# Layer 0's masked row maxima: a fused add-and-minimum on the Vector engine in place of mask products on the Tensor engine

## The chip, the cores and the metric

The kernel runs on one NeuronCore of a Trainium2 chip. A core has a Tensor engine (TensorE, PE in the profile; PEld is its weight loads), a Vector engine (DVE), a Scalar engine (ACT), a GpSimd engine (POOL) and a Sync engine (SP) that issues transfers. Products land in PSUM, which has eight banks of 128 partitions x 512 fp32 columns; everything else lives in SBUF. Each engine works through its own instructions in order and waits on semaphores for the others. The metric is the device time of one execution in microseconds; the time shown is the median of three runs.

## The reference, cut to what matters

The program is four layers over `x`, 16 batches of 256 tokens with 256 features. Layer 0 is self-attention with rotated queries and keys and a mask, cross-attention to 77 context tokens with a mask, and an MLP; layer 1 is a cross-attention; layer 2 is self-attention, cross-attention and an MLP; layer 3 is rotated self-attention, cross-attention and an MLP. All attentions have 16 heads of 16 features. The part that the change touches is the softmax of layer 0's self-attention:

```python
s = jnp.einsum('bqhd,bkhd->bhqk', q, k) * scale
s = jnp.where(mask, s, jnp.finfo(s.dtype).min)
a = jax.nn.softmax(s, axis=-1)
```

The mask is one 256 x 256 array of booleans, the same for all batches and heads. A softmax needs, for each query and head, the maximum of its masked scores over the 256 keys.

## The kernel before

**Stages.** `pixart_kernel` walks through the layers: stage "a" (layer 0's self-attention) and "ac" (its cross-attention), the MLP "b", then "cx", "c" and "cc" (layers 1 and 2), the MLP "d", then "e" and "ec" (layer 3) and the MLP "f". Each stage works on 16 batches, and `x` stays in SBUF. The function `attention` makes the tasks of one batch. It is called for every stage and takes `masked=True` only for "a" and "ac"; the stages "a", "c" and "e" are self-attentions (`self_` is true), and "a" and "e" rotate queries and keys.

**One self-attention batch.** Normalised `x` is turned, projected to queries and keys, rotated on DVE and POOL (lines 588 to 608), turned back (line 628) and copied out as `qT` and `kz`. `kz` holds the keys twice, with one of the two heads of each 32-row strip zeroed, so that one product of a 32-row strip gives the scores of two heads. Heads come in two groups `g` of eight (four strips of two heads), queries in two tiles `t` of 128. The strips are taken in two row pairs `rp`.

*Maxima.* For each `g`, `t` and `rp` one PE task (`begin`, line 734) takes two PSUM banks, one for each strip of the pair. In stage a it first writes the mask into both banks: the bf16 identity times the bf16 mask `mb`, 512 columns (the mask twice), line 740. `mb` is 0 where the mask is true and -2^120 where it is false. Then it adds the scores by a 32-row product of 512 columns, line 749. For each bank one DVE task reduces 128 x 512 to two negated maxima a row (line 772) and writes them into `mxt`. So there are 2 x 2 x 4 = 16 reductions a batch. When a group's eight are done, `mxt` is turned on PE (line 787) and put into the extended queries `qx` on DVE (line 792), where the maximum becomes an extra feature of the query.

*Exponentials.* The scores are computed a second time, keys in rows now and the maximum subtracted by the product itself (`begin`, line 821; product at line 834). The turned mask `mbT` is written into the banks first (line 827). ACT takes the exponential (line 848). The values product (line 857) sums over keys. DVE transposes the result (line 866), takes reciprocals (line 873), POOL multiplies, DVE transposes back (line 883), and the output projection follows (line 904), with the gate (line 917) and the residual (line 920).

**What sets the order.** No loop order is issued as it stands. Every step is a task with an engine, an estimated duration, dependencies and buffers, added to an `Order`; `solve` (line 101) plays a list schedule over these estimates, and the kernel issues the tasks in the order that comes out. `CAPS` gives the buffers of each kind: 8 banks ("b"), 2 maxima tiles, 4 batches' queries and keys. PE takes the ready task with the lowest priority number; the other engines take tasks that hold a bank first, then by the time at which they became ready. Two PE tasks that use different row pairs are started together and their products alternate (`choose`), since they use different rows of the array; `begin` of `Order` (line 125) gives such a pair one common duration, the longer of the two. In stage a the mask products raise both kinds of task, maxima and exponentials, from 0.864 to 1.614 in these estimates. Batches are admitted to an attention stage in the order in which they became ready.

The mask tiles `mb`, `mbT` and `kbm` (for "ac") live in a buffer of the kind "ctx", made at line 988 and the lines after it.

Of the kernel before, what the change touches and what calls it, by code (L numbers as in the profile page):

```python
# [10 lines left out]
F32 = mybir.dt.float32  # L11
# [6 lines left out]
P = 128  # L18
# [41 lines left out]

class Task:
    __slots__ = ("eng", "dur", "run", "deps", "take", "prio", "rp", "left", "ready", "outs", "held", "start", "end", "no", "since", "kind", "joins",
                 "line", "last")


class Hold:
# [7 lines left out]
class Order:  # L74
# [8 lines left out]
        self.caps, self.tasks = caps, []  # L83

    def add(self, eng, dur, run, deps=(), take=(), use=(), prio=0, rp=None, kind=None, joins=(),
            line=None, last=True):

        t = Task()
        t.joins, t.line, t.last = joins, line, last
        t.eng, t.dur, t.run, t.prio, t.rp, t.kind = eng, dur, run, prio, rp, kind  # L90
        t.deps = [d for d in deps if d is not None]
        t.take, t.held = list(take), list(take) + list(use)
        for h in t.held:
            h.users += 1
        t.outs, t.left, t.ready, t.no, t.since = [], len(t.deps), 0.0, len(self.tasks), None
        for d in t.deps:
            d.outs.append(t)
        self.tasks.append(t)
        return t

    def solve(self):
# [22 lines left out]

        def begin(ts):
            nonlocal seq, mode
            dur = max(t.dur for t in ts)
            if ts[0].eng == "PE":
                kind = "row" if ts[0].rp is not None else ts[0].kind
                dur += self.TURN.get(kind, 0.2) if kind != mode else 0.0  # L130
                mode = kind
            for t in ts:
                for h in t.take:
                    h.no = loose[h.tag].pop(0) if h.tag in loose else taken[h.tag]
                    taken[h.tag] += 1
                for name, key in t.joins:
                    lines.setdefault(name, []).append(key)
                if t.line is not None and t.last:
                    lines[t.line[0]].pop(0)
                t.start, t.end = now, now + dur  # L140
                waiting[t.eng].remove(t)
                seq += 1
                heapq.heappush(events, (now + dur, seq, t))
            if ts[0].eng != "NO":
                free[ts[0].eng] = now + dur
            result.append((now, len(result), ts))
# [60 lines left out]
def pixart_kernel(ctx: ExitStack, tc: tile.TileContext, x, cond_t, ctx_in, mask_c, mask_s, tables, vecs, rows,  # L207
# [427 lines left out]
    def attention(b, name, n, wv, wkeys, h_w, w_t, eps, mod, half, biases, masked, pre_add, gate, prio, ctxs=None,  # L635
# [85 lines left out]
        for g in range(NC):  # L721
            h_mx, h_x = Hold("mx"), Hold("qx")

            def open_mx(g=g):
                s["mx", g] = mxs[state["mx"] % len(mxs)]
                state["mx"] += 1
            t_mx = add("NO", 0.0, open_mx, deps=[q_t, k_t], take=[h_mx], prio=prio, line=("mx", (nm, g)))
            red = []
            for t in tiles:
                for rp in range(2):  # L730
                    hs = [Hold("b"), Hold("b")]
                    u = {}

                    def begin(g=g, t=t, rp=rp, u=u, hs=hs):
                        lists = []
                        for i in range(2):
                            r = 2 * rp + i
                            ps = u[i] = psum(hs[i])
                            if self_ and masked:
                                nc.tensor.matmul(ps.rearrange("p (s k) -> p s k", k=N), lhsT=identb,  # L740
                                                 rhs=mb[:, t, :].unsqueeze(1).to_broadcast([P, 2, N]),
                                                 start=True, stop=False)
                        for i in range(2):
                            r = 2 * rp + i
                            R = slice(32 * r, 32 * r + 32)
                            ps, ls = u[i], []
                            keys = s["kz"][R, g].rearrange("p s k -> p (s k)")
                            if self_:
                                ls.append(lambda ps=ps, R=R, keys=keys: nc.tensor.matmul(  # L749
                                    ps, lhsT=s["qT"][R, g, t * P:(t + 1) * P], rhs=keys,  # L750
                                    start=not masked, stop=True))
                            else:
                                pv = ps[:, 0:4 * n].rearrange("p (u k) -> p u k", k=n)
                                if masked:
                                    ls.append(lambda pv=pv, r=r: nc.tensor.matmul(
                                        pv, lhsT=onesb[32 * r:32 * r + 1, :],
                                        rhs=kbm[32 * r:32 * r + 1, b, :].unsqueeze(1).to_broadcast([1, 4, LC]),
                                        start=True, stop=False))
                                for tt in range(NT):
                                    ls.append(lambda ps=ps, R=R, keys=keys, tt=tt: nc.tensor.matmul(  # L760
                                        ps[:, 2 * tt * n:2 * (tt + 1) * n], lhsT=s["qT"][R, g, tt * P:(tt + 1) * P],
                                        rhs=keys, start=not masked, stop=not masked or tt == NT - 1))
                            lists.append(ls)
                        return lists
                    dur = 2 * MM if self_ else 0.55
                    a = add("PE", dur + (0.75 if self_ and masked else 0.0), begin, deps=[t_mx], take=hs,
                            use=[h_q, h_k, h_mx, *h_masks], prio=prio, rp=rp, kind="m")
                    for i in range(2):
                        def reduce(g=g, t=t, r=2 * rp + i, i=i, u=u):
                            m = s["mx", g]  # L770
                            if self_:
                                nc.vector.tensor_reduce(m[:, t, 32 * r:32 * r + 17:16],  # L772
                                                        u[i].rearrange("p (s k) -> p s k", k=N), AX.X, ALU.max,
                                                        negate=True)
                            else:
                                nc.vector.tensor_reduce(m[:, :, 32 * r:32 * r + 17:16],  # L776
                                                        u[i][:, 0:4 * n].rearrange("p (t s k) -> p t s k", s=2, k=n),
                                                        AX.X, ALU.max, negate=True)
                        red.append(add("DVE", 0.69 if self_ else 0.46, reduce, deps=[a], use=[hs[i], h_mx],
                                       prio=prio))  # L780
            hm, u2 = Hold("b"), {}

            def turn(g=g, u2=u2, hm=hm):
                u2["p"] = psum(hm)
                s["qx", g] = work.tile([P, 2, N], F32, tag="qx", bufs=CAPS["qx"], name=f"qx_{nm}_{g}")
                for t in range(NT):
                    nc.tensor.transpose(u2["p"][:, t * P:(t + 1) * P], s["mx", g][:, t, :], ident)  # L787

            def plus(g=g, u2=u2):
                qx = s["qx", g]  # L790
                for i in range(2):
                    nc.vector.scalar_tensor_tensor(qx[:, i, :], u2["p"][:, 0:N], spot[:, i:i + 1], s["qT"][:, g, :],
                                                   ALU.mult, ALU.add)
            a = add("PE", 2 * TR, turn, deps=red, take=[hm, h_x], use=[h_mx], prio=prio, line=("qx", (nm, g)))
            qx_t.append(add("DVE", 0.85, plus, deps=[a], use=[hm, h_x, h_q], prio=prio))
            h_qx.append(h_x)
# [7 lines left out]
        for g in range(NC):  # L804
            u5, h_av, h_so = {}, Hold("b"), Hold("ts")
            for kc in range(nk):
# [10 lines left out]
                for rp in (1, 0):  # L817
# [3 lines left out]
                    def begin(g=g, kc=kc, rp=rp, u=u, hs=hs):  # L821
# [8 lines left out]
                        for i in range(2):  # L830
# [6 lines left out]
                                    start=not (self_ and masked), stop=not (self_ and masked) or q == 1))  # L837
                                for q in range(2)])
                        return lists
                    a = add("PE", 2 * MM + (0.75 if self_ and masked else 0.0), begin,  # L840
                            deps=[t_e, k_t], take=hs, use=[h_k, h_qx[g], *h_masks], prio=prio, rp=rp, kind="e")
                    for i in range(2):
                        def exp(g=g, kc=kc, r=2 * rp + i, i=i, u=u):
# [143 lines left out]

    mask_t = work.tile([P, NC, CT], F32, tag="ctxT", bufs=CAPS["ctx"], name="ctxT_masks")
    mask_b = mask_t.rearrange("p c n -> p (c n)")[:, 0:1152].bitcast(BF16)
    mb, mbT = (mask_b[:, i * 512:(i + 1) * 512].rearrange("p (t n) -> p t n", n=N) for i in range(2))  # L990
    kbm = mask_b[:, 1024:1024 + CT].rearrange("p (b n) -> p b n", n=LC)

# [240 lines left out]
```

## Time and profile before

| | |
|---|---|
| median of three runs | 2854.78 us (2854.26 to 2854.85) |
| profiled execution | 2851.73 us, its span 2849.3 us |
| mean granted TensorE clock in it | 0.993 |
| PE busy | 2782.7 us, 98% of the span |
| DVE busy | 1651.1 us, 58% |
| ACT busy | 1205.4 us, 42% |
| POOL busy | 1062.6 us, 37% |
| line 740, mask products of the maxima | 256, 380 ns each in their rows |
| line 827, mask products of the exponentials | 256, 382 ns each |
| line 772, reductions, all three self-attentions | 768, 684 ns each |

How to read it: the profile is one execution. A busy PE is not a PE at its peak, since products are pipelined and the ends of their rows are modelled: rows overlap, so that the distance from one start to the next is shorter than a row. The same holds on DVE, where the next instruction starts some 70 to 80 ns before the row ahead of it ends. The span is the time from the first to the last instruction; the execution's own time has 2.4 us around it. Idle time of an engine that is not the bound costs nothing.

### The profile page before, as it was taken

The numbers are of one execution on the slowest core, as the hardware profiler recorded it, in microseconds if no ns is written. First come the engines' busy times: TensorE is split into PE (matmuls) and PEld (weight loads), VectorE is DVE, ScalarE is ACT, GpSimd is POOL, SyncE is SP. The second block draws the span as 40 slices with busy tenths as digits, with TensorE's granted clock in tenths as the row PEclk, the third lists the DMA queues.
The fourth block names the chain that finished last, engine by engine and source line by source line (L and its number), as shares of the span: only waits on it lengthen the run. The fifth ranks groups of instructions, "written<-read, shape, count | busy, mean of one in ns | idle before, by whom it ended". The sixth has DMA issues, their size and how long they took to land.

```text
span 2849.3 us, 55972 instructions
## 1 busy us (share of the span) xinstructions
PE 2782.7 (98%) x22560; PEld 1954.0 (69%) x22560; DVE 1651.1 (58%) x4042; ACT 1205.4 (42%) x2496; POOL 1062.6 (37%) x1414
## 2 busy tenths in 40 slices
PE   7999999999999999999999998999999999999999
PEld 4555555667788766656666666888656666666888
DVE  4656666677322267787777677111678888786110
ACT  1333343455333245545555554222444454443222
POOL 2332322254544444323333544343333333354331
PEclk9999999999999999999999999999999999999999
DMA  4010000000111100010000000100000000000000
GB/s 169 23 31 5 5 7 5 9 11 17 60 34 42 56 19 2 5 28 12 15 14 13 5 2 1 63 19 15 31 1 1 1 2 1 1 2 1 23 19 19
DMA packets 32034, 56.24 MB, mean 20 GB/s; under 512 B 3456, under 2 KB 22128, under 8 KB 31008
## 3 DMA queue, kind: packets, MB, share of 16 engines
q1 hardware_dynamic: 31776, 52.68, 5.8%
q8 instruction: 177, 2.90, 0.4%
q14 instruction: 81, 0.66, 0.1%
HBM read 48.34 MB, written 4.33 MB: 18 GB/s over the span
## 4 chain that ended last, share of the span: by engine, by line
PE 90%; DVE 4%; POOL 3%; ACT 1%; issue 1%; DMA 1%; SPq 0%; DVEq 0%; ACTq 0%; POOLq 0%
PE bank L904 18%; PE bank L834 12%; PE bank L947 12%; PE bank L857 11%; PE bank L749 7%; PE bank L540 6%; PE bank L588 5%; PE bank L706 5%; PE bank L451 3%; PE bank L787 2%; PE bank L827 2%; PE bank L760 2%; PE bank L740 2%; PE bank L628 1%; DVE mxt L772 1%
## 5 line engine op out<-in xcount | busy, mean ns | idle before, releaser
L772 DVE TENSOR_REDUCE mxt<-bank 128x2 f32<-128x512 f32 x768 | 484.8, 684 | 149.5 <-PE bank L749 138.5
L776 DVE TENSOR_REDUCE mxt<-bank 128x4 f32<-128x308 f32 x512 | 211.8, 470 | 35.4 <-PE bank L834 18.6
L848 ACT ACTIVATE e_a<-bank 128x512 f32<-128x512 f32 x256 | 136.7, 598 | 209.8 <-PE bank L749 147.0
L848 ACT ACTIVATE e_e<-bank 128x512 f32<-128x512 f32 x256 | 136.3, 603 | 161.9 <-PE bank L749 80.7
L848 ACT ACTIVATE e_c<-bank 128x512 f32<-128x512 f32 x256 | 135.6, 600 | 119.9 <-PE bank L749 83.6
L910 DVE TENSOR_TENSOR x_sb<-x_sb,bank 128x512 f32<-128x512 f32 x80 | 54.8, 685 | 189.1 <-PE bank L904 187.1
L749 PE MATMUL bank<-kz_c,qT_c 32*128 32x512 f32 x512 | 142.0, 627 | 0.0
L749 PE MATMUL bank<-kz_e,qT_e 32*128 32x512 f32 x512 | 137.0, 632 | 1.5 <-DVE kz_e L563 0.8
L834 PE MATMUL bank<-qx_e,kz_e 32*128 32x256 f32 x1024 | 134.6, 402 | 0.0
L834 PE MATMUL bank<-qx_c,kz_c 32*128 32x256 f32 x1024 | 132.5, 397 | 0.0
L834 PE MATMUL bank<-qx_a,kz_a 32*128 32x256 f32 x1024 | 122.6, 400 | 0.0
L749 PE MATMUL bank<-kz_a,qT_a 32*128 32x512 f32 x512 | 120.9, 640 | 0.0
L952 ACT ACTIVATE h_f<-bank,vec 128x256 f32<-128x256 f32 x128 | 53.5, 470 | 153.5 <-PE bank L947 132.5
L952 ACT ACTIVATE h_d<-bank,vec 128x256 f32<-128x256 f32 x128 | 53.5, 470 | 153.6 <-PE bank L947 132.5
L947 PE MATMUL bank<-xT_b,w_b 128*128 128x256 f32 x512 | 114.6, 380 | 0.0
L904 PE MATMUL bank<-w_b,h_b 128*128 128x256 f32 x512 | 113.7, 379 | 0.0
L904 PE MATMUL bank<-w_d,h_d 128*128 128x256 f32 x512 | 113.4, 380 | 0.0
L947 PE MATMUL bank<-xT_d,w_d 128*128 128x256 f32 x512 | 113.4, 380 | 0.0
L947 PE MATMUL bank<-xT_f,w_f 128*128 128x256 f32 x512 | 113.4, 380 | 0.0
L904 PE MATMUL bank<-w_f,h_f 128*128 128x256 f32 x512 | 113.2, 379 | 0.0
L714 ACT COPY vt<-bank 128x256 f32<-128x256 f32 (+1 forms) x160 | 54.7, 374 | 129.2 <-PE bank L706 118.1
L952 ACT ACTIVATE h_b<-bank,vec 128x256 f32<-128x256 f32 x128 | 53.5, 470 | 125.7 <-PE bank L947 83.4
(386 smaller groups left out, 6788.3 us busy)
## 6 DMA issues: line engine op xcount, KB each, us to landing
cin<-in_ctx_in_dram SPq DMA_DIRECT2D x36, 128.0 KB, 2.1
x_sb<-in_x_dram SPq DMA_DIRECT2D x16, 256.0 KB, 6.3
gb_b<-gate_g0m SPq DMA_DIRECT2D x16, 256.0 KB, 3.3
gb_c<-gate_g2a SPq DMA_DIRECT2D x16, 256.0 KB, 3.2
gb_d<-gate_g2m SPq DMA_DIRECT2D x16, 256.0 KB, 3.1
out_dram<-x_sb SPq DMA_DIRECT2D x16, 256.0 KB, 2.1
w_c<-in_wc_dram SPq DMA_DIRECT2D x1, 3072.0 KB, 9.9
w_e<-in_we_dram SPq DMA_DIRECT2D x1, 3072.0 KB, 10.1
```

Source lines behind the costliest of these rows:

```text
L540: nc.tensor.matmul(dst[:, g, :], lhsT=w[:, k, g * P:(g + 1) * P], rhs=xT[:, k, :], start=(k == 0), stop=(k == NC - 1))
L588: nc.tensor.matmul(u["p"][0:r, at:at + D], lhsT=xT()[:, k, t * P:t * P + r], rhs=w()[:, k, :], start=(k == 0), stop=(k == NC - 1))
L706: nc.tensor.matmul(ps[0:rows_n, t * D:(t + 1) * D], lhsT=xT[:, k, t * P:t * P + rows_n], rhs=wv[kv][:, k, :], start=(k == 0), stop=(k == N ...
L749: ls.append(lambda ps=ps, R=R, keys=keys: nc.tensor.matmul(ps, lhsT=s["qT"][R, g, t * P:(t + 1) * P], rhs=keys, start=not masked, stop=True))
L772: nc.vector.tensor_reduce(m[:, t, 32 * r:32 * r + 17:16], u[i].rearrange("p (s k) -> p s k", k=N), AX.X, ALU.max, negate=True)
L776: nc.vector.tensor_reduce(m[:, :, 32 * r:32 * r + 17:16], u[i][:, 0:4 * n].rearrange("p (t s k) -> p t s k", s=2, k=n), AX.X, ALU.max, neg ...
L834: (lambda ps=u[i], R=R, q=q: nc.tensor.matmul(ps[0:rows_n, q * N:(q + 1) * N], lhsT=s["kz"][R, g, q, kc * P:kc * P + rows_n], rhs=s["qx", ...
L848: nc.scalar.activation(e, u[i][0:rows_n], AF.Exp)
L857: nc.tensor.matmul(u5["p"][32 * r:32 * r + 32, 1 - q, :], lhsT=s["v"][0:rows_n, kc, 8 * g + 2 * r + 1 - q, :], rhs=s["e", g, kc, r][0:rows ...
L904: nc.tensor.matmul(u["p"][:, t, :], lhsT=lhsT(k, t), rhs=w()[:, k, :], start=(k == 0), stop=(k == nk - 1))
L947: nc.tensor.matmul(u["p"][:, j, :], lhsT=wv["w1"][:, k, f * P:(f + 1) * P], rhs=s["xT"][:, k, :], start=(k == 0), stop=(k == NC - 1))
L952: nc.scalar.activation(s["h", i][:, j, :], u["p"][:, j, :], func, bias=vcol(b1, 2 * i + j))
```

## The change

In stage a's maxima the mask products (line 740) go, and the score product starts its bank itself. In place of one reduction over both heads' 512 columns, DVE runs, for each head, `tensor_tensor_reduce` over 256 columns: it adds the mask tile `mb` (bf16, SBUF) to the scores (fp32, PSUM), multiplies by -1, writes the result to a scratch tile `junk`, and writes the minimum of it, started at 3e38, into the head's place in `mxt`. That is the negated maximum of the masked scores, as before. The masks of the exponentials stay on PE. The planner's estimates follow: the maxima task loses its 0.75, a masked reduction is estimated at 0.95 in place of 0.69, and a masked exponentials task carries 0.62 in a new field `more`, which is added for each task of a pair where the old 0.75 stood inside the longer task's duration.

```diff
@@ class Task, Order.add @@
-                 "line", "last")
+                 "line", "last", "more")
...
-            line=None, last=True):
+            line=None, last=True, more=0.0):
...
-        t.joins, t.line, t.last = joins, line, last
+        t.joins, t.line, t.last, t.more = joins, line, last, more
@@ Order.solve, begin @@
-            dur = max(t.dur for t in ts)
+            dur = max(t.dur for t in ts) + sum(t.more for t in ts)
@@ attention, maxima @@
                             ps = u[i] = psum(hs[i])
-                            if self_ and masked:
-                                nc.tensor.matmul(ps.rearrange("p (s k) -> p s k", k=N), lhsT=identb,
-                                                 rhs=mb[:, t, :].unsqueeze(1).to_broadcast([P, 2, N]),
-                                                 start=True, stop=False)
...
                                 ls.append(lambda ps=ps, R=R, keys=keys: nc.tensor.matmul(
                                     ps, lhsT=s["qT"][R, g, t * P:(t + 1) * P], rhs=keys,
-                                    start=not masked, stop=True))
+                                    start=True, stop=True))
...
                     dur = 2 * MM if self_ else 0.55
-                    a = add("PE", dur + (0.75 if self_ and masked else 0.0), begin, deps=[t_mx], take=hs,
+                    a = add("PE", dur, begin, deps=[t_mx], take=hs,
                             use=[h_q, h_k, h_mx, *h_masks], prio=prio, rp=rp, kind="m")
...
                             m = s["mx", g]
-                            if self_:
+                            if self_ and masked:
+                                for i2 in range(2):
+                                    nc.vector.tensor_tensor_reduce(
+                                        junk, u[i][:, i2 * N:(i2 + 1) * N], mb[:, t, :], -1.0, 3.0e38, ALU.add, ALU.min,
+                                        m[:, t, 32 * r + 16 * i2:32 * r + 16 * i2 + 1])
+                            elif self_:
                                 nc.vector.tensor_reduce(m[:, t, 32 * r:32 * r + 17:16],
                                                         u[i].rearrange("p (s k) -> p s k", k=N), AX.X, ALU.max,
                                                         negate=True)
...
-                        red.append(add("DVE", 0.69 if self_ else 0.46, reduce, deps=[a], use=[hs[i], h_mx],
+                        red.append(add("DVE", 0.95 if self_ and masked else 0.69 if self_ else 0.46, reduce, deps=[a], use=[hs[i], h_mx],
                                        prio=prio))
@@ attention, exponentials @@
-                    a = add("PE", 2 * MM + (0.75 if self_ and masked else 0.0), begin,
+                    a = add("PE", 2 * MM, begin, more=0.62 if self_ and masked else 0.0,
                             deps=[t_e, k_t], take=hs, use=[h_k, h_qx[g], *h_masks], prio=prio, rp=rp, kind="e")
@@ set-up @@
+    junk = const.tile([P, N], F32, name="junk")
```

## The prediction

> **What bounds the kernel now.** I read the page's busy shares first, then the chain of waits over the layer-0 self-attention, then windows of steady work, then single groups. The page gives the engines over the whole span:
>
> ```profile
> PE 2782.7 (98%) x22560; PEld 1954.0 (69%) x22560; DVE 1651.1 (58%) x4042; ACT 1205.4 (42%) x2496; POOL 1062.6 (37%) x1414
> ```
>
> TensorE is the bound nearly everywhere, so the question is whether it stays so in the stage that changes. That is the self-attention "a" of layer 0. The first and last starts of its maxima products (line 749), beside those of layer 3's "e", which has the same rotated queries and keys but no mask, are:
>
> ```profile
> L749 PE MATMUL bank<-kz_a,qT_a x512: 587/640/692, 49.7 to 532.0; 32*128 32x512 f32 x171
> ...
> L749 PE MATMUL bank<-kz_e,qT_e x512: 587/588/692, 2017.8 to 2382.6; 32*128 32x512 f32 x171
> ```
>
> Stage a takes 482.3 us for 16 batches, stage e 364.8. The chain that ended last, between 48 and 548 us, is TensorE work almost only:
>
> ```profile
> by line: PE bank L834 15.6%; PE bank L857 13.0%; PE bank L827 12.6%; PE bank L749 11.8%; PE bank L588 10.9%; PE bank L740 10.6%; PE bank L706 5.8%; PE bank L904 5.7%; PE bank L628 2.8%; PE bank L787 2.0%; PE bank L451 1.6%; PE bank L540 1.6
> ```
>
> Line 740 is the mask product that the change removes: 10.6% of 500 us is 53 us of the chain. Line 827, the mask of the exponentials, stays. Windows of steady stage a, of steady stage e, and of the two stages' starts (columns: window, length, then PE, PEld, DVE, ACT, POOL busy):
>
> ```profile
> 98.00:498.00 400.00, 398.98 (x3185) 231.77 (x3183) 256.71 (x539) 148.20 (x289) 114.67 (x145) 1.00 0.03 10
> 2150.00:2350.00 200.00, 199.91 (x1809) 132.36 (x1808) 167.55 (x355) 99.05 (x195) 66.58 (x89) 1.00 0.01 1
> 48.00:98.00 50.00, 48.83 (x395) 25.11 (x394) 33.29 (x70) 19.14 (x40) 12.72 (x17) 1.00 0.15 43
> 2000.00:2100.00 100.00, 95.20 (x676) 60.70 (x676) 74.95 (x149) 35.39 (x69) 30.80 (x33) 0.98 0.06 22
> ```
>
> In steady a PE idles 1.0 us of 400 while DVE is 64% busy; in steady e PE idles 0.1 of 200 while DVE is 84% busy. So a DVE at 84% does not yet starve TensorE in this pipeline with its eight banks.
>
> **What the Trainium skill says.** "Vector Engine (DVE) Microarchitecture Reference", section "Measured stream behaviour on trn2", gives 1.0417 ns per column plus about 75 ns per instruction back to back: 608 ns for 512 columns. The trace agrees: two reductions take 1.29 us and one 0.684, a pitch of 0.605. "VectorE: DVE Perf Modes", section "The perf-mode tier table", has two-source operations and any PSUM operand in fp32 at one element per cycle, so the new operation can't be faster per column. The same page, "Two Vector instructions with no wait between them", says that an operation that writes out its accumulator is two instructions, the second an accumulator read. No row of this trace has such a pair, so its price is open. "TensorE: Matmul & The Clock Gate", section "Wait — 56ns, not 53.3ns?", has 215.7 ns from start to start for bf16 products of 512 columns; four masks in a row take 1.03 us here with 0.379 for each one, so (1.03 - 0.379)/3 = 0.217.
>
> **The change, part by part.**
> *Removed:* 16 batches x 2 groups x 2 tiles x 4 row strips = 256 mask products (line 740) with their weight loads. Floor: 256 x 0.217 = 55.6 us. Stage e has none of a's 512 masks (740 and 827), so (482.3 - 364.8)/512 = 0.229 us each with the change of weights and of array shape around them; I take that: 256 x 0.229 = 58.6. A group of four alone takes 0.96 to the next product's start, 0.24 each: ceiling 61.4. Nothing hides this work.
>
> *Added on DVE:* each of 256 reductions over 128x512 becomes two fused operations over 128x256, one operand in PSUM, one bf16 in SBUF. The nearest rows, in a stretch of DVE's timeline:
>
> ```profile
> 402.10 0.87 DVE L792 SCALAR_TENSOR_TENSOR qx_a<-bank,spot,qT_a 128x256 f32<-128x256 f32 x2
> 403.07 0.69 DVE L600 TENSOR_TENSOR qk_a<-bank,tabT 128x512 f32<-128x512 f32 x1
> 403.68 0.75 DVE L603 TENSOR_TENSOR r_qk_a<-bank,tabT 128x256 f32<-128x256 f32 x2
> ```
>
> One of line 603 has 0.414, so its pitch is 0.75 - 0.414 = 0.336; line 792, with 0.470 for one, has 0.40. Low end, no separate accumulator read: 2 x 0.336 = 0.67 for a pair, against 0.605 now. A gain on DVE is excluded: the same 512 columns at the same rate and one more start. A read priced as this trace's short operations (two reciprocals over 8 elements: 0.27 us with 0.164 for one, pitch 0.11) adds 0.22: 0.89 to 1.02. High end, a program of two cycles per column: 2 x (512 x 1.0417 + 75) + 0.22 = 1.44. I take 0.92, +0.315 each: 256 x 0.315 = 81 us of DVE work.
>
> *Does it fit?* The steady 400 us hold 208 reductions, 13 batches: 400/13 = 30.8 us a batch, DVE 256.71/13 = 19.75. After: PE 30.8 - 16 x 0.229 = 27.1, DVE 19.75 + 16 x 0.315 = 24.8, 91%. That is above the 84% that e carries without a stall. DVE binds from (27.1 - 19.75)/16 = 0.46 extra, a pair of 1.07 us. So the 81 us are costed at nothing because 36% of DVE's time is idle in the stage; without that cover they would cost all 81. For 84 to 91% I charge 5 us of stalls, an estimate between 0 and twice that: behind a longer reduction stand the rotation (lines 600 and 603, which POOL's sum and the turn-back of line 628 wait for), the transposes of line 866 that free a values bank, and the two banks of its own pair, held about 0.6 us longer. Another attention's work can't fill such a gap: cross-attention "ac" first shows at about 518 us.
>
> *The start:* before e's pipeline is full PE idles 4.8 us (2000 to 2100); a's start loses 1.2 because masks kept PE longer. Without them it should look like e's: 4 us charged.
>
> *Planner:* the new costs (0.95 on DVE; 0.62 per masked exponential task of a pair, in place of 0.75 for the whole pair) change the order that is written out, in stage a alone so far as costs go; later stages keep their tasks. I count nothing: the same row products share the array, and a pair with two masks less needs 2 x 0.217 = 0.43 us less, which the new costs follow. No DMA or queue issue is added or moved; the scratch tile "junk" is written by DVE alone and read by nobody. No wait for another engine is added.
>
> *Sum:* -58.6 + 5 + 4 = -49.6. The profiled execution took 2851.73 (span 2849.3), so it becomes 2802.1; the median of the runs shown, 2854.78, stands 3.05 above it, which gives **2805**.
>
> **Rivals.**
> *DVE becomes the bound of stage a.* A pair near 1.15 gives 19.75 + 16 x 0.545 = 28.5 us a batch: 16 x (30.8 - 28.5) = 37 saved, less 9 of start and stalls: 2827. For it: DVE is the busiest engine behind PE here and a fused program is in no row of this trace. Against: short operations are cheap on it.
> *Slower: the fused program runs at half rate.* It decides from DVE 30.8 us a batch, a pair of 0.605 + (30.8 - 19.75)/16 = 1.30 us. At 1.44 it is 33.1 a batch: 16 x 2.3 + 9 = +46, 2901. For it: two streams and an accumulator in one instruction. Against: one stream comes from PSUM, and rows of that kind (line 603) run at full rate.
> *The gain isn't there:* stalls move to the exponentials (their banks wait for maxima that come late) and the order gives back what was saved; 2855. Against it: e does the same with 84% on DVE and no idle PE.
>
> **How the numbers follow.** Forecast, PE-bound, 0.68 (own range 2794 to 2815: saved 55.6 to 61.4, charges 0 to about 15). DVE-bound 0.17. Half rate 0.09. Nothing left 0.03. Other small gains 0.03. Faster by over 0.2% (5.7 us, about what a measurement can tell from no change): 0.68 + 0.17 + 0.03 = 0.88; same 0.03; slower 0.09. The range 2794 to 2840 holds the forecast and most of the DVE-bound case, about 0.82; the half-rate case, which holds the upper bound of the price, is the part left out.
>
> **What would show it.** Right: no line 740; line 749's a-products end near 482 us; DVE 85 to 93% busy in steady a with PE idle under 2%; a pair of fused rows with its reads every 0.85 to 1.0 us; from the MLP on everything earlier by one offset. Wrong: a pair over 1.07 us, or PE waiting on the maxima in steady a; the prediction fails by its DVE price, not by the TensorE part.

## The result, and the profile after

The changed kernel takes 2842.07 us (median of five runs, 2841.21 to 2843.65) against 2854.66 for the kernel before on the same chip: 12.6 us less, a ratio of 0.9957 with a 95% interval of 0.9943 to 0.9972. The prediction was 2805, a gain of 50, and the upper end of its range 2840. The profiled execution took 2841.21 us, its span 2839.3, at a mean granted clock of 0.989.

Line numbers shift by one below the new code: the maxima product is line 745 now, the fused operation line 769, the reduction of the unmasked stages line 773. The page's busy time of each engine, and its two costliest groups on DVE's maxima (line, engine, operation, shapes | busy us, mean ns of one | idle time ahead of them and what ended it):

```profile
PE 2762.6 (97%) x22304; PEld 1939.7 (68%) x22304; DVE 1702.4 (60%) x4810; ACT 1207.3 (43%) x2496; POOL 1064.9 (38%) x1414
...
L773 DVE TENSOR_REDUCE mxt<-bank 128x2 f32<-128x512 f32 x512 | 322.3, 682 | 54.6 <-PE bank L745 50.8
L769 DVE CUSTOM_DVE_ANT_0 junk<-bank,ctxT_masks 128x256 f32<-128x256 f32 x512 | 215.7, 421 | 49.0 <-PE bank L745 14.0
```

The 256 mask products of the maxima are gone (PE has 22304 products in place of 22560), and 512 fused operations of 421 ns stand on DVE. The first and last starts of the maxima products of stages a and e:

```profile
L745 PE MATMUL bank<-kz_a,qT_a x512: 587/692/1218, 48.2 to 511.7; 32*128 32x512 f32 x171
...
L745 PE MATMUL bank<-kz_e,qT_e x512: 587/587/692, 2008.3 to 2373.0; 32*128 32x512 f32 x171
```

Stage a's take 463.5 us, 18.8 less than before, where the forecast had them end near 482 us, 50 earlier than before. Stage e takes 364.7, as before. The MLP b's products (before the change, and after it):

```profile
L947 PE MATMUL bank<-xT_b,w_b x512: 378/379/484, 736.2 to 969.0; 128*128 128x256 f32 x171
...
L948 PE MATMUL bank<-xT_b,w_b x512: 379/379/483, 725.8 to 959.1; 128*128 128x256 f32 x171
```

They start 10.4 us earlier, and stage e's first maxima product 9.5, so what was gained and lost lies ahead of b. The chain of waits between 48 and 548 us now has DVE in it:

```profile
by line: PE bank L835 14.5%; PE bank L745 14.0%; PE bank L858 12.3%; PE bank L828 11.0%; PE bank L588 8.2%; DVE junk L769 7.7%; PE bank L905 5.1%; PE bank L706 4.7%; issue 2.7%; PE bank L628 2.3%; PE bank L788 2.0%; PE bank L540 1.9%; PE ba
```

The fused operation carries 7.7% of these 500 us itself, and the maxima products have grown from 11.8 to 14.0%. Nothing was added to these products. Part of the growth is waiting for banks that DVE has yet to free: the fused operations are named for 7.3 us of idle time ahead of line 745, in 18 waits. Part may be a lower clock (a stretch with both is shown at the end). Windows of the stage (window, length, then PE, PEld, DVE, ACT, POOL busy, granted TensorE clock, share of the DMA engines, GB/s):

```profile
98.00:498.00 400.00, 390.71 (x3062) 229.22 (x3061) 306.60 (x1193) 155.18 (x302) 121.99 (x153) 0.98 0.04 10
...
48.00:98.00 50.00, 47.40 (x337) 24.05 (x336) 37.78 (x158) 17.00 (x37) 7.45 (x10) 0.90 0.16 45
...
148.00:198.00 50.00, 49.54 (x362) 26.95 (x360) 36.57 (x152) 16.65 (x32) 9.91 (x15) 0.86 0.10 27
```

PE is idle for 9.3 us of the 400, where it was 1.0 before, and its clock is below 1.00 in some windows; before, it was 1.00 in all of them. DVE's 306.60 is only 77%, which would not look like a bound. DVE's timeline says why that figure misleads (start, length):

```profile
212.43 0.42 DVE L769 CUSTOM_DVE_ANT_0 junk<-bank,ctxT_masks 128x256 f32<-128x256 f32 x1
212.78 0.08 DVE L769 DVE_READ_ACCUMULATOR2_ANT mxt<- 128x1 f32 x1
213.01 0.42 DVE L769 CUSTOM_DVE_ANT_0 junk<-bank,ctxT_masks 128x256 f32<-128x256 f32 x1
213.36 0.08 DVE L769 DVE_READ_ACCUMULATOR2_ANT mxt<- 128x1 f32 x1
213.47 0.42 DVE L769 CUSTOM_DVE_ANT_0 junk<-bank,ctxT_masks 128x256 f32<-128x256 f32 x1
213.82 0.08 DVE L769 DVE_READ_ACCUMULATOR2_ANT mxt<- 128x1 f32 x1
214.05 0.42 DVE L769 CUSTOM_DVE_ANT_0 junk<-bank,ctxT_masks 128x256 f32<-128x256 f32 x1
```

The operations of one strip start 0.46 us apart (213.01, 213.47), and the next strip's follows 0.58 later (214.05): a pair takes 1.04 us. Most of the 428 fused operations between 98 and 498 us that follow another one sit at these two distances (0.46 to 0.47 and 0.57 to 0.58). An operation with its read covers 0.43 us, so a pair's rows cover 0.86, and 0.18 of each pair is counted neither as busy nor as a wait with a releaser. With 214 pairs that is at most 38.5 us, and DVE's occupied time is up to 306.6 + 38.5 = 345, 86% of the window.

What fills the gap is in the instructions. The listing of DVE's queue with its waits (buffer numbers left out):

```
before   L772 TensorReduce mxt<-bank 128x2                  [waits PE]
after    L769 fused add-min junk,mxt<-bank,mask 128x256     [waits DVE, PE]
         L769 accumulator read mxt 128x1
         L769 fused add-min junk,mxt<-bank,mask 128x256     [waits DVE]
         L769 accumulator read mxt 128x1
```

All but 25 of the 512 fused operations wait on DVE's own semaphore. All of them write the one tile `junk`, so each has to be told that the writer before it has finished, and that writer is the operation just ahead. It is the accumulator read, the second of its two rows, that raises the semaphore: in the timeline a read ends at 213.44 (213.36 + 0.08) and the next operation of its strip starts at 213.47. The first of a strip also waits for PE; where it waits for two semaphores, a separate semaphore instruction often stands ahead of it (231 of them on line 769, 55 on the reduction's line before).

### The profile page after: what moved, and what is told of

Read it like the earlier page. It is cut to its first block, busy times and chain, and to the rows that moved or that the text cites. A ratio compares the mean times of both kernels' runs of the same rounds, so it can differ in the third digit from the quotient of the medians.

```text
span 2839.3 us, 56433 instructions
## 1 busy us (share of the span) xinstructions
PE 2762.6 (97%) x22304; PEld 1939.7 (68%) x22304; DVE 1702.4 (60%) x4810; ACT 1207.3 (43%) x2496; POOL 1064.9 (38%) x1414
## 4 chain that ended last, share of the span: by engine, by line
PE 87%; DVE 6%; POOL 3%; issue 1%; ACT 1%; DMA 1%; SPq 0%; DVEq 0%; POOLq 0%; ACTq 0%
PE bank L905 18%; PE bank L835 12%; PE bank L948 12%; PE bank L858 11%; PE bank L745 7%; PE bank L540 6%; PE bank L588 5%; PE bank L706 5%; PE bank L451 2%; PE bank L788 2%; PE bank L756 2%; PE bank L828 2%; DVE junk L769 1%; PE bank L628 1%; DVE mxt L773 1%
## 5 line engine op out<-in xcount | busy, mean ns | idle before, releaser
L773 DVE TENSOR_REDUCE mxt<-bank 128x2 f32<-128x512 f32 x512 | 322.3, 682 | 54.6 <-PE bank L745 50.8
L769 DVE CUSTOM_DVE_ANT_0 junk<-bank,ctxT_masks 128x256 f32<-128x256 f32 x512 | 215.7, 421 | 49.0 <-PE bank L745 14.0
L745 PE MATMUL bank<-kz_a,qT_a 32*128 32x512 f32 x512 | 141.5, 670 | 0.1
L835 PEld LDWEIGHTS bank<-qx_a,kz_a 32*128 32x128 f32 x1024 | 75.9, 190 | 52.3 <-issue 46.1
```

Of the source, the lines that this page charges most:

```text
L745: ls.append(lambda ps=ps, R=R, keys=keys: nc.tensor.matmul(ps, lhsT=s["qT"][R, g, t * P:(t + 1) * P], rhs=keys, start=True, stop=True))
L769: nc.vector.tensor_tensor_reduce(junk, u[i][:, i2 * N:(i2 + 1) * N], mb[:, t, :], -1.0, 3.0e38, ALU.add, ALU.min, m[:, t, 32 * r + 16 * i2 ...
L773: nc.vector.tensor_reduce(m[:, t, 32 * r:32 * r + 17:16], u[i].rearrange("p (s k) -> p s k", k=N), AX.X, ALU.max, negate=True)
L835: (lambda ps=u[i], R=R, q=q: nc.tensor.matmul(ps[0:rows_n, q * N:(q + 1) * N], lhsT=s["kz"][R, g, q, kc * P:kc * P + rows_n], rhs=s["qx", ...
```

## The experiments

**The theory** after the result: the waits on `junk` make a pair 1.04 us, and DVE's load goes to 98% of PE's. By the prediction's own numbers that is 19.75 + 16 x (1.04 - 0.605) = 26.7 us a batch against PE's 27.1. **The rivals:** the order that the planner writes with its new estimates; and the TensorE part being worth less than thought. Eleven kernels tell them apart. Ratios are to the kernel before on the same chip, with 95% intervals.

### The TensorE part alone

Stage a's maxima are taken of the unmasked scores, by the plain reduction, estimated at 0.69 as in the other stages.

```diff
-                            if self_ and masked:
-                                for i2 in range(2):
-                                    nc.vector.tensor_tensor_reduce(...)
-                            elif self_:
+                            if self_:
...
-  red.append(add("DVE", 0.95 if self_ and masked else 0.69 if self_ else 0.46, reduce, ...
+  red.append(add("DVE", 0.69 if self_ else 0.46, reduce, ...
```

> Leaves the mask out of layer 0's maxima: no mask product, no fused operation, the plain reduction over 512 columns stays (softmax is shifted by the maximum of the unmasked scores; the masks of the exponentials stay). The planner's costs of the changed kernel, but 0.69 for this reduction. It measures the TensorE part of the sum alone. Theory D (DVE's price took the gain): 55 to 60 us saved less about 4 at the start, 2797 to 2805. Theory O (the order that the planner writes out stalls PE by itself once the mask products are gone): clearly above that, 2815 to 2840. Rival: the gain never was there, within 6 us of 2842.

It took 2804.71 us, 0.9823 (0.9808 to 0.9837): 50.0 us less than before. Its maxima products by source line, and its steady window:

```profile
L745 PE MATMUL bank<-kz_a,qT_a x512: 587/588/1217, 48.1 to 473.6; 32*128 32x512 f32 x171
```

```profile
98.00:498.00 400.00, 399.36 (x3419) 240.69 (x3422) 284.64 (x605) 168.16 (x325) 128.08 (x163) 1.00 0.04 11
```

PE is idle for 0.6 us of 400 and the clock is 1.00. The removed masks are worth nearly what they were thought to be worth (this kernel's order differs from that before, so the order's own part is in the 50.0), and the 37.4 us by which the change falls short are to be found in the DVE operation and the order.

### The order, with one scratch tile

Three kernels keep the change's operations and alter the planner's estimates alone, so they issue the same work in another order. The first has the three estimates of the kernel before.

```diff
-  a = add("PE", dur, begin, deps=[t_mx], ...
+  a = add("PE", dur + (0.75 if self_ and masked else 0.0), begin, deps=[t_mx], ...
...
-  red.append(add("DVE", 0.95 if self_ and masked else 0.69 if self_ else 0.46, reduce, ...
+  red.append(add("DVE", 0.69 if self_ else 0.46, reduce, ...
...
-  a = add("PE", 2 * MM, begin, more=0.62 if self_ and masked else 0.0, ...
+  a = add("PE", 2 * MM + (0.75 if self_ and masked else 0.0), begin, ...
```

> The changed kernel's instructions, but the planner's three costs of the kernel before, so that the tasks come in the order of before. Theory D: DVE has the same work (a pair of fused operations each 1.05 us or so), so the time stays near the changed kernel's, 2836 to 2850. Theory O: the order of before mixes maxima with other work no worse, and most of the removed 58 us shows, 2800 to 2825.

2847.54 us, 0.9974 (0.9963 to 0.9985).

The second takes the pair's measured 1.05 as DVE's estimate.

```diff
-  red.append(add("DVE", 0.95 if self_ and masked else ...
+  red.append(add("DVE", 1.05 if self_ and masked else ...
```

> The changed kernel, with 1.05 in place of 0.95 as the planner's cost of a masked reduction: what the trace shows for a pair with its two reads and its waits. Theory D: no gain from a better estimate, 2838 to 2848. Theory O: a change of more than 6 us, either way, from the order alone.

2879.65 us, 1.009 (1.0073 to 1.0106): slower than before, by telling the planner the truth. The order alone costs 37.6 us beside the change. The third takes 0.69, and so issues its tasks in the order of the unmasked kernel above.

```diff
-  red.append(add("DVE", 0.95 if self_ and masked else 0.69 if self_ else 0.46, reduce, ...
+  red.append(add("DVE", 0.69 if self_ else 0.46, reduce, ...
```

> The changed kernel's instructions in the order of the unmasked experiment: 0.69 in place of 0.95 as the planner's cost of a masked reduction. Beside that experiment (2804.7) only the fused operations are added, so the difference is DVE's price at one and the same order; beside the changed kernel the order alone. If DVE's work alone took the gain: 2835 to 2850, 30 to 45 us over the unmasked one. If the order of the changed kernel took it: 2806 to 2825.

2835.97 us, 0.9932 (0.9915 to 0.9948). At this one order the unmasked kernel takes 2804.71, so the fused operations cost 31.3 us there, and the change's own order adds the other 6.1 (the intervals of these two overlap at their ends, so the 6.1 is rough). The order matters, but none of the three brings the gain back.

### Half of the pairs

Only the first strip of each row pair is fused. The second keeps its mask product and its plain reduction.

```diff
+                            if self_ and masked and i == 1:
+                                nc.tensor.matmul(ps.rearrange("p (s k) -> p s k", k=N), lhsT=identb,
+                                                 rhs=mb[:, t, :].unsqueeze(1).to_broadcast([P, 2, N]),
+                                                 start=True, stop=False)
...
-                            if self_ and masked:
+                            if self_ and masked and i == 0:
                                 for i2 in range(2):
...
-  red.append(add("DVE", 0.95 if self_ and masked else ...
+  red.append(add("DVE", 1.05 if self_ and masked and i == 0 else ...
```

The second strip's score product keeps `start=False`, and a maxima task carries `more=0.31`.

> Only one strip of each row pair takes its mask by the fused operation; the other keeps its mask product and its plain reduction. Planner: 1.05 for a fused reduction, 0.69 for a plain one, 0.31 added for the one mask product left in a maxima task. PE loses half of 58.6, DVE gains 8 x 0.445 = 3.6 us a batch, 23.3 of 28.9, 81%. Theory D: DVE no longer binds, 29 less 4 saved, 2828 to 2834. Theory O: no such rule; anywhere from 2825 to 2850, set by the order that comes out.

2833.70 us, 0.9928 (0.9913 to 0.9943). Half of the masks taken off PE give 21 us, and all of them 12.6: the second half of the masks costs more on DVE than it frees on PE. That speaks for DVE as the limit, though the order differs here too.

### The wait on the scratch tile

The result goes to four tiles in turn, so that an operation waits for the one four before it. Nothing else changes; the planner's estimates and the order are those of the change.

```diff
-                                        junk, u[i][:, i2 * N:(i2 + 1) * N], mb[:, t, :], -1.0, 3.0e38, ALU.add, ALU.min,
+                                        junks[2 * i + i2], u[i][:, i2 * N:(i2 + 1) * N], mb[:, t, :], -1.0, 3.0e38, ALU.add, ALU.min,
...
-    junk = const.tile([P, N], F32, name="junk")
+    junks = [const.tile([P, N], F32, name=f"junk{j}") for j in range(4)]
```

> The changed kernel with four scratch tiles in turn: an operation waits for the fourth operation before it, which has long ended, and not for the one just ahead. Theory W: a pair of 0.85 to 0.95, time 2810 to 2830. Theory P: a pair of 1.0 or more, 2837 to 2848.

2814.52 us, 0.9864 (0.9849 to 0.9878): 27.6 us below the change. DVE's timeline:

```profile
350.95 0.42 DVE L769 CUSTOM_DVE_ANT_0 junk<-bank,ctxT_masks 128x256 f32<-128x256 f32 x1
351.29 0.08 DVE L769 DVE_READ_ACCUMULATOR2_ANT mxt<- 128x1 f32 x1
351.29 0.42 DVE L769 CUSTOM_DVE_ANT_0 junk<-bank,ctxT_masks 128x256 f32<-128x256 f32 x1
351.63 0.08 DVE L769 DVE_READ_ACCUMULATOR2_ANT mxt<- 128x1 f32 x1
351.63 0.42 DVE L769 CUSTOM_DVE_ANT_0 junk<-bank,ctxT_masks 128x256 f32<-128x256 f32 x1
```

The rows are as long as ever (0.42 and 0.08), but they start 0.34 us apart, within a strip and between strips alike. The next operation starts together with the read of the one ahead. A pair takes 0.69 us, not 1.04. The waits on DVE's semaphore are still in the queue, only for an operation that has long finished, and 198 separate semaphore instructions are still there too: neither costs anything by itself. What cost 0.35 us a pair is the wait for the operation just ahead. The Trainium skill's "Vector Engine (DVE) Microarchitecture Reference", section "Measured stream behaviour on trn2", prices built-in operations; an estimate from its figures for 256 columns is 256 x 1.0417 + 75 = 342 ns, and the fused operation's 0.34 agrees. "VectorE: DVE Perf Modes", section "The DRAIN you can't avoid", says of a chain of copies that a semaphore after each costs nothing extra. The four tiles agree, since each operation raises one here too. What the section does not price is the wait for the operation just ahead: it cost 0.12 us within a strip and 0.24 between strips. Why it is twice as much between strips, where a second wait stands, no run shows.

Two tiles, one for each operation of a strip, ask whether it is really the one just ahead:

```diff
-                                        junk, u[i][...
+                                        junks[i2], u[i][...
```

> Two scratch tiles, one for each head, planner's costs of the changed kernel: an operation waits for the one before the last. Theory W in the strict form (only the wait for the operation just ahead stalls, because it has not ended): as with four, 2811 to 2818, a pair of 0.69 to 0.75. If any wait on DVE's own semaphore stalls, or the operation before the last has not signalled yet: a pair of 0.8 or more and 2820 to 2842.

2815.88 us, 0.9869 (0.9854 to 0.9884), with the same 0.34 between starts:

```profile
356.76 0.42 DVE L769 CUSTOM_DVE_ANT_0 junk<-bank,ctxT_masks 128x256 f32<-128x256 f32 x1
357.11 0.08 DVE L769 DVE_READ_ACCUMULATOR2_ANT mxt<- 128x1 f32 x1
357.11 0.42 DVE L769 CUSTOM_DVE_ANT_0 junk<-bank,ctxT_masks 128x256 f32<-128x256 f32 x1
```

A wait for the second operation back is free here; only the one just ahead is late.

### The result written over its own bank

Without a scratch tile, the fused operation writes its result over the scores that it read. The first of a strip then writes a bank that no DVE operation has just written; the second still waits for the first.

```diff
-                                        junk, u[i][:, i2 * N:(i2 + 1) * N], mb[:, t, :], ...
+                                        u[i][:, i2 * N:(i2 + 1) * N], u[i][:, i2 * N:(i2 + 1) * N], mb[:, t, :], ...
```

> The changed kernel, but the fused operation writes its unused result back over the scores in the bank, not to the one scratch tile. Then the first operation of a pair no longer waits for DVE's own last instruction, and one of the two waits of that kind, and the extra semaphore instruction before it, go. Planner's costs as in the changed kernel. Theory W (the waits on the one scratch tile make the pair 1.05 us long): a pair of about 0.95, DVE 25.3 us of work a batch against 27.1, the time 2815 to 2832. Theory P (the price is in the two operations and their reads themselves): a pair of 1.0 or more, 2837 to 2848.

2829.14 us, 0.9918 (0.9903 to 0.9933). Its timeline:

```profile
351.10 0.43 DVE L769 CUSTOM_DVE_ANT_0 bank<-bank,ctxT_masks 128x256 f32<-128x256 f32 x1
351.45 0.14 DVE L769 DVE_READ_ACCUMULATOR2_ANT mxt<- 128x1 f32 x1
351.45 0.47 DVE L769 CUSTOM_DVE_ANT_0 bank<-bank,ctxT_masks 128x256 f32<-128x256 f32 x1
```

The operation that begins a strip (351.45) starts 0.35 after the one ahead. The second of a strip comes 0.53 after the first (350.57 to 351.10), and most of the others 0.56. The read is longer here, 142 ns in place of 82, and its end is what the second operation waits for: it ends at 351.06 (350.92 + 0.14), and that operation starts at 351.10. A pair is about 0.91 us, and the time lies between those of one scratch tile and of four. The same with the planner's 0.69:

```diff
-                                        junk, u[i][:, i2 * N:(i2 + 1) * N], mb[:, t, :], ...
+                                        u[i][:, i2 * N:(i2 + 1) * N], u[i][:, i2 * N:(i2 + 1) * N], mb[:, t, :], ...
...
-  red.append(add("DVE", 0.95 if self_ and masked else 0.69 if self_ else 0.46, reduce, ...
+  red.append(add("DVE", 0.69 if self_ else 0.46, reduce, ...
```

> The in-place result and the planner's 0.69 together. If both the waits and the order count: below either alone, 2806 to 2820. If DVE's work binds whatever the order: as the in-place run.

2823.73 us, 0.9897 (0.9882 to 0.9911). That is below either edit alone, though above the 2806 to 2820 expected, and its interval overlaps that of the in-place run.

### Four tiles, and the two other orders

Four scratch tiles with the planner's 0.69:

```diff
-                                        junk, u[i][...
+                                        junks[2 * i + i2], u[i][...
...
-  red.append(add("DVE", 0.95 if self_ and masked else 0.69 if self_ else 0.46, reduce, ...
+  red.append(add("DVE", 0.69 if self_ else 0.46, reduce, ...
```

> Four scratch tiles and the planner's cost of a masked reduction at 0.69, which is what a pair took in the run with four scratch tiles (two operations and two reads every 0.69 us). The order is that of the unmasked experiment (2804.7). Theory W, and the planner now told the truth: DVE does 16 x 0.085 = 1.4 us more a batch than there and has room, 2803 to 2811. If the fused operations cost time by themselves although DVE has room: 2812 or more, as with four scratch tiles and 0.95.

2805.07 us (2804.37 to 2807.77), 0.9833 (0.9818 to 0.9848). With the masks in place it is the fastest kernel of the study: 48.9 us below the kernel before, 37.0 below the change. Its steady window:

```profile
98.00:498.00 400.00, 399.47 (x3405) 241.27 (x3407) 301.76 (x1276) 168.03 (x325) 127.79 (x162) 1.00 0.04 11
```

PE is full again while DVE does all of the masked maxima. The unmasked kernel, which has this order and no masks in the maxima at all, took 2804.71: without the waits the fused operations cost nothing that stands out from the spread of the runs, some 3 to 5 us.

Four tiles with the planner's 1.05, the order that was the worst with one tile:

```diff
-                                        junk, u[i][...
+                                        junks[2 * i + i2], u[i][...
...
-  red.append(add("DVE", 0.95 if self_ and masked else ...
+  red.append(add("DVE", 1.05 if self_ and masked else ...
```

> Four scratch tiles with the planner's cost at 1.05, the order of the 2879.7 run with one scratch tile. If the loss of that order came from DVE being full (each burst of maxima stalls TensorE for as long as DVE is behind): most of it goes, 2812 to 2828. If the order is bad for TensorE by itself: 2845 or more.

2854.22 us, 1.0 (0.9992 to 1.0009). The same operations without their stalls, in another order, give all of the gain back. Its windows:

```profile
248.00:298.00 50.00, 49.69 (x419) 29.08 (x414) 31.45 (x130) 20.79 (x42) 18.14 (x24) 1.00 0.02 7
298.00:348.00 50.00, 43.99 (x294) 23.76 (x293) 44.55 (x211) 12.78 (x24) 7.73 (x11) 0.91 0.00 1
348.00:398.00 50.00, 50.00 (x410) 29.73 (x410) 23.61 (x83) 21.66 (x44) 21.31 (x27) 0.96 0.04 9
```

DVE's work comes in bursts: 44.55 of 50 us busy while PE idles 6, then 23.61. In the middle window the output projection waits 5.1 us at once for the transposes of line 884 on DVE. So this order is bad even without the stalls. Why a longer estimate makes the list schedule bunch the maxima in this way was not followed through the schedule, and stays open.

All times at one glance, by the pair's price on DVE and by the planner's estimate of it:

| | pair, us | 0.69 | 0.95 | 1.05 |
|---|---|---|---|---|
| unmasked, plain reduction | 0.605 | 2804.7 | | |
| fused, two scratch tiles | 0.69 | | 2815.9 | |
| fused, four scratch tiles | 0.69 | 2805.1 | 2814.5 | 2854.2 |
| fused, in place | 0.91 | 2823.7 | 2829.1 | |
| fused, one scratch tile | 1.04 | 2836.0 | 2842.1 (the change) | 2879.7 |

## Why the prediction was wrong, step by step

*Removed* was right in kind, and a little large. With no work added on DVE, masks and start together came to -50.0 where the steps have -58.6 + 4 = -54.6. The 4.6 between them is within what an order is worth, and no run parts the two.

*The start* was right in size by luck, in another form than foreseen. The window in the four-tile kernel with 0.69:

```profile
48.00:98.00 50.00, 48.53 (x384) 25.47 (x383) 33.87 (x156) 20.00 (x41) 8.41 (x13) 0.93 0.16 45
```

PE is busy about as long as before (48.83), where idle time had been foreseen. But the granted clock is 0.93 where it was 1.00: at most 0.07 x 50 = 3.5 us of TensorE time, against the 4 charged.

*Added on DVE* is the step that failed first. The pair was put at 0.92 us, between 0.67 and 1.44; it measured 1.04. The term itself was composed wrongly too. The accumulator read, which was to add 0.22, adds nothing when nobody waits for it: without the waits a pair takes 0.69, at the low end. What made it 1.04 stands in the sentence on the planner and the buffers: "the scratch tile 'junk' is written by DVE alone and read by nobody. No wait for another engine is added." That is true, and it was the wrong question. The added wait is for DVE itself, on its own last write, and it costs 0.35 us a pair. At the order of the unmasked kernel it is worth 2835.97 - 2805.07 = 30.9 us, at the change's own order 27.6.

*Does it fit?* failed as well, and here lies the term of the sum that was off most: 5 us charged for stalls, 31.3 measured. The price alone does not explain it, since 1.04 is still below the 1.07 at which DVE was to bind. The in-place kernels have just about the pair of 0.92 that was assumed (0.91, DVE at (19.75 + 16 x 0.305)/27.1 = 91% of PE). They cost 18.7 us more than four tiles at one order and 14.6 at the other, where 5 had been charged and 10 was the most. That stage e runs with DVE at 84% and PE full did not show what happens at 91%. At the change's 98% the loss is already 31. At the one order of 0.69 the time above the unmasked kernel is 0.4 us for a pair of 0.69, 19.0 for 0.91 and 31.3 for 1.04 (the middle one also writes to another place): these three show no edge at which DVE starts to bind, but a slope that begins well before it. That the four-tile kernel comes out at just the 2805 of the forecast is luck: it gained 4.6 us less on TensorE (50.0 for 54.6) and lost 4.6 less on DVE (0.4 for 5) than in the sum.

*Planner* failed: "I count nothing". Its reason did not hold either. The pair that loses two masks (one maxima and one exponentials task) goes from 1.614 to 0.864 + 0.62 = 1.484 in the estimates, 0.13 less and not 0.43; and a pair of two exponentials tasks, which loses none, goes up by 0.49. With unchanged operations the orders lie 49 us apart with four tiles, and 44 with one. For the change itself, the new estimates cost about 6 us against the best order tried, and gain some 5 against the old estimates (2847.5); both are rough, since the intervals overlap.

*The sum*, put right with the measured terms: -50.0 for masks and start, +31.3 for the fused operations with their waits, +6.1 for the order, is -12.6. The terms are differences of measured times along one path of kernels, so they add up by construction.

*The rivals.* "DVE becomes the bound" is the one that came true, in kind, with a pair of 1.04 rather than 1.15. Its time of 2827 was too low; it too charged only 9 us for start and stalls together, and nothing for the order. The half-rate program is excluded, since the operation runs at 0.34 us for 256 columns. "The gain isn't there" is not what happened to the change, but the kernel with 1.05 and four tiles gives all of it back, by its order.

*The signs* given in advance worked in part. The pair of 1.04 lies between the bands for right (0.85 to 1.0) and wrong (over 1.07) and so decides nothing. PE's waits in steady a did point at DVE: it idles 9.3 of 400 us, 2.3% where under 2% was the sign of being right, and for 7.3 of them the operations of line 769 are named. The maxima that end at 511.7 and not near 482 did say that the forecast had failed, and from the MLP on everything was earlier by one offset, as foreseen. The band of "DVE 85 to 93% busy" would have misled, because the rows show 77% and the time of a wait on the engine itself is in no row.

## What to carry to other kernels

Before an operation with an output that nobody reads is added, ask what its next instance must wait for: give such outputs at least two tiles in turn, so that the wait is for an operation that has finished. Look for waits of an engine on itself in the instructions or in the distance between starts, since busy time doesn't show them and the list of waits hardly does (2.1 us in 10 waits of line 769 on itself in the change). When an operation's cost is changed in a planner, measure the new order apart from the operation: here the operation's true cost gave the worst order with one scratch tile (1.05) and the best with four (0.69), of those tried.

## What was not expected of the hardware

Some stretches in which TensorE waited were followed by a lower granted clock. In the change, DVE works through a long run of maxima from 148 us on, and from 155 us PE's products are held up behind it. PE's timeline shows 16 maxima products in one stretch of 5.90 us:

```profile
158.51 5.90 PE L745 MATMUL bank<-kz_a,qT_a 32*128 32x512 f32 x16
```

The windows around it:

```profile
153.00:158.00 5.00, 5.00 (x41) 2.65 (x37) 4.11 (x20) 0.68 (x2) 0.00 (x0) 1.00 0.39 105
158.00:163.00 5.00, 5.00 (x20) 3.07 (x20) 4.68 (x20) 0.00 (x0) 0.00 (x0) 0.63 0.37 107
163.00:168.00 5.00, 5.00 (x17) 1.89 (x14) 4.11 (x21) 0.02 (x1) 0.00 (x0) 0.50 0.00 0
168.00:173.00 5.00, 5.00 (x26) 2.39 (x26) 4.43 (x20) 2.15 (x4) 0.00 (x0) 0.51 0.00 0
173.00:178.00 5.00, 5.00 (x54) 2.37 (x48) 3.45 (x19) 2.17 (x4) 0.00 (x0) 1.00 0.01 3
```

PE counts as busy in all of it, but does 17 products in 5 us at half the clock, and it takes until about 173 us to be at 1.00 again. Not every wait has this after it: later in the same kernel PE idles 1.34 of 5 us, and the clock stays at 1.00.

```profile
225.00:230.00 5.00, 3.66 (x29) 1.92 (x28) 4.35 (x19) 1.38 (x2) 0.00 (x0) 1.00 0.00 0
```

What makes the difference no run shows. The Trainium skill's "TensorE: Matmul & The Clock Gate", section "A second HAM failure mode: psum-queue depth-cycling", tells of a kernel whose products pause between groups as they cycle through PSUM banks, and whose clock falls to half and comes back; this trace agrees, with a clock of 0.50. The prediction had left it out: a DVE that is late can cost twice, by the wait and by the clock behind it. Over the windows of 50 us from 48 to 548, the clock that is missing comes to (0.10 + 0.14 + 0.03) x 50 = 13.5 us in the change, none in the kernel before, and 21.5 in the four-tile kernel with 1.05. That is about the most that the lower clock can have cost directly, since a PE that waits loses nothing by it. Nor is it all: the four-tile kernel with the change's own order is at 1.00 in all ten windows and still takes 9.5 us more than the one with 0.69. No run here takes the clock apart from the waits that precede its fall. The executions of one kernel, with the same instructions in the same order, give a hint that the clock counts: of the twelve of the four-tile kernel with 1.05, the ten at a mean clock of 0.984 took 2852.6 to 2855.5 us and the two at 0.986 took 2849.6 and 2849.8.

Beside that: a fused operation with an accumulator is two rows, and its read is wholly hidden behind the next operation when nothing makes that operation wait. The Trainium skill's "VectorE: DVE Perf Modes", section "Two Vector instructions with no wait between them", names the two instructions, and the trace shows both. The read's row grows from 82 to 142 ns where the operation's other output goes to PSUM.
